# A fused Perceiver layer on one core: the attention's weight sums taken earlier on GpSimd and copied later, and a finer first load

## The chip, the core and the metric

The kernel runs on one core of a Trainium2 chip. The core has five engines with instruction streams of their own: TensorE (PE in the profile, with its weight loads as PEld) multiplies matrices, VectorE (DVE) and ScalarE (ACT) work on elements, GpSimd (POOL) does so too, and SyncE (SP) here issues DMAs. Engines wait for each other through semaphores. The metric is the device time of one execution in microseconds (us), lower is better.

## What is computed

The reference is one layer of three blocks on x (256 x 512, fp32): cross attention over 4096 context tokens and the 256 tokens themselves, a state-space block, and a mixture of experts. The change touches only the attention, cut to:

```python
q = rms_norm((ln(x) @ wq).reshape(256, 16, 128), q_norm_w)
k = rms_norm((ln(x) @ wk).reshape(256, 4, 128), k_norm_w)
v = (ln(x) @ wv).reshape(256, 4, 128)
k_ctx = rms_norm((ctx @ wk_ctx).reshape(4096, 4, 128), k_norm_w)
v_ctx = (ctx @ wv_ctx).reshape(4096, 4, 128)
q, k = rope(q), rope(k)
# keys and values of the context first, then those of x (causal)
x = x + softmax(q @ k_full.T / sqrt(128) + mask) @ v_full @ wo
```

`ln` is a layer norm without weights; 16 query heads share 4 key heads.

## The kernel before, in words

Everything is fp32. The 256 tokens are two tiles (`t`) of 128; the context is eight chunks (`c`) of 512 tokens, each of four pieces of 128.

**Loads.** SP issues the first transfers in the order written: the first piece of the first context chunk (`ctx0`, L88), the context keys' weights `wkc` in two transfers of two 128-row slices (L90 to 91), `x_sb` (L92), the rest of `ctx0` (L93, L94), and the context values' weights `wvc` (L95). `wkc` and `wvc` are the two halves of one tile `wkv`. Then come `wk`, `wq` in four column blocks, and `wv`, each in a slot of a pool of six (`wpool`, L131).

**Start.** `layernorm(t)` (L187) takes mean and variance on DVE and the inverse root on POOL (`power_half`, L181, whose POOL line is L185), then writes `xn`. Three pieces of context keys are projected (`key_piece`, L278), `xn` is transposed through PSUM into `xT` (`turn_xn`, L197), and two tables for the rotary embedding go to the first quarter of `oacc` (L388). `oacc` is the array in which the attention's output is accumulated later; its first such write is at L536.

**Queries and keys of x.** `self_block` (L429) multiplies a tile of `xT` with 512 columns of weights (PE, `ps_self`), copies the result to `raw` and squares it (ACT, L404 and L242), applies the tables (DVE, L409 to L412), and scales it by the inverse root (POOL: `r` at L185, then L413). The result is transposed (`selfT`, L437) two steps of the list at L456 later. A query block is named here by its column block and its tile, (2,1) for instance; the last, (3,0) and (3,1), end just ahead of the attention.

**Attention.** `bounded_attention` (L496) runs over stages: stage 0 for the keys of x, then one stage for each chunk. A pass of scores (`scT`, L512), the exponential on ACT, for the diagonal tiles a mask on DVE (L518), row sums on DVE, then the product with the values (`oT`, L532). In stages 1 to 7, keys and values of the next chunk are projected between these passes by a Strassen-like scheme with seven products for eight (`fast_steps`, L310). It needs four sums of blocks of the weights, T1 to T4, and four sums of blocks of each chunk, S1 to S4, all taken on POOL. `fast_weights` (L297) takes three slots of `wpool`, and writes T1, T2, T4 there and T3 in place over a block of `wkv` (L305 to L308). S1 to S4 are at L320 to L323.

**What sets the order.** A scheduler places each engine's instructions from a model of when their inputs and slots are ready; what an engine has in its stream it does in that order. SP's stream holds most DMAs, and a DMA also waits for the one that used its semaphore before it, of which there are eight.

Of the kernel before, what the change touches and what calls it, by code (L numbers as in the profile page):

```python
# [15 lines left out]
ALU = mybir.AluOpType  # L16
# [3 lines left out]
P = 128  # L20
L = 256
NT = L // P
DM = 512
KD = DM // P
T = 4096
CK = 512
NC = T // CK
NH = 16
NKV = 4
REP = NH // NKV  # L30
HD = 128
# [29 lines left out]
def rope_tables():  # L61
    inv = (1.0 / np.float32(THETA) ** (np.arange(0, HD, 2, dtype=np.float32) / np.float32(HD))).astype(np.float32)
    freqs = np.outer(np.arange(L, dtype=np.float32), inv).astype(np.float32)
    return np.stack([np.cos(freqs), np.sin(freqs)], axis=1).astype(np.float32)
# [3 lines left out]
def perceiver_layer(ctx: ExitStack, tc: tile.TileContext, a: dict, out: bass.AP):  # L68
    nc = tc.nc
    V, S, G, TE = nc.vector, nc.scalar, nc.gpsimd, nc.tensor  # L70
# [12 lines left out]
    wkv = early.tile([P, 2, KD, 512], FP, name="wkv")  # L83
    wkc, wvc = wkv[:, 0], wkv[:, 1]
    ctx0 = early.tile([P, CK // P, KD, P], FP, name="ctx0")


    load_ctx0 = lambda i, n: nc.sync.dma_start(ctx0[:, i:i + n], a["ctxT"][0, :, i:i + n])  # L88
    load_ctx0(0, 1)
    for k in range(0, KD, 2):  # L90
        nc.sync.dma_start(wkc[:, k:k + 2, :], a["wk_ctx"][k * P:(k + 2) * P, :].rearrange("(k p) n -> p k n", p=P))
    nc.sync.dma_start(x_sb, a["x"].rearrange("(t p) d -> p t d", p=P))  # L92
    load_ctx0(1, 1)  # L93
    load_ctx0(2, 2)  # L94
# [12 lines left out]
    mhalf = const.tile([P, NH], FP, name="mhalf")  # L107
# [21 lines left out]
    def layer(ctx, bounded):  # L129
# [8 lines left out]
        oacc = keep.tile([P, NT, NKV, REP * P], FP, name="oacc")  # L138
# [10 lines left out]
        def carve(tl, *shapes):  # L149

            dims = " ".join(f"d{i}" for i in range(len(tl.shape) - 1))
            tl = tl if len(tl.shape) == 2 else tl.rearrange(f"p {dims} -> p ({dims})")
            out, at = [], 0
            for shape in shapes:
                n = int(np.prod(shape))
                v = tl[:, at:at + n]
                at += n
                if len(shape) == 2:
                    v = v.rearrange("p (a b) -> p a b", b=shape[1])
                elif len(shape) == 3:  # L160
                    v = v.rearrange("p (a b c) -> p a b c", b=shape[1], c=shape[2])
                out.append(v)
            assert at <= tl.shape[1]
            return out
# [9 lines left out]
        def wpiece(src, name):  # L174

            n = src.shape[1]
            w = wpool.tile([P, KD, 512], FP, tag="w", name=name)
            nc.sync.dma_start(w[:, :, :n], src.rearrange("(k p) n -> p k n", p=P))
            return w

        def power_half(dst, src, scale, eps, n):  # L181

            v = small.tile([P, NH], FP, tag="pv", name="pv")
            V.tensor_scalar(v[:, :n], src, scale, eps, ALU.mult, ALU.add)  # L184
            G.tensor_tensor(dst, v[:, :n], mhalf[:, :n], ALU.pow)  # L185

        def layernorm(t):  # L187

            st = small.tile([P, 6], FP, tag="bn", name="bn")
            V.bn_stats(st, x_sb[:, t, :])  # L190
            mv = small.tile([P, 2], FP, tag="mv", name="mv")
            V.bn_aggr(mv, st)
            rs = small.tile([P, 1], FP, tag="rs", name="rs")
            power_half(rs, mv[:, 1:2], 1.0, 1e-5, 1)
            V.tensor_scalar(xn[:, t, :], x_sb[:, t, :], mv[:, 0:1], rs, ALU.subtract, ALU.mult)

        def turn_xn(t, tp):  # L197

            for k in range(KD):
                TE.transpose(tp[:, k * P:(k + 1) * P], xn[:, t, k * P:(k + 1) * P], ident)  # L200
            V.tensor_copy(xT[:, :, t * P:(t + 1) * P], tp.rearrange("p (k n) -> p k n", k=KD))
# [43 lines left out]
        def key_rms(raw, r):  # L245


            ss = head_squares(raw)
            if bounded:
                power_half(r, ss, 1.0, HD * 1e-6, NKV)  # L250
            else:
                power_half(r, ss, 1.0 / HD, 1e-6, NKV)
                G.tensor_tensor(raw, raw, r.unsqueeze(2).to_broadcast([P, NKV, HD]), ALU.mult)
# [40 lines left out]

        fast = {}

        def fast_weights():  # L297
            fw = [wpool.tile([P, KD, 512], FP, tag="w", name=f"fast{i}") for i in range(3)]
            T = (2, 2, 256)
            fast["T2"], fast["T4"] = carve(fw[0], T, T)  # L300
            fast["S2"], fast["S4"], fast["u3"], fast["u2"] = carve(fw[1], (2, 2, P), (2, 2, P), (2, 256), (2, 256))

            fast["T1"], fast["S1"], fast["S3"] = carve(fw[2], T, (2, 2, P), (2, 2, P))
            b11, b12, b21, b22 = (wkv[:, :, k:k + 2, n:n + 256] for k in (0, 2) for n in (0, 256))
            G.tensor_tensor(fast["T1"], b12, b11, ALU.subtract)  # L305
            G.tensor_tensor(fast["T2"], b22, fast["T1"], ALU.subtract)
            G.tensor_tensor(fast["T4"], b21, fast["T2"], ALU.subtract)
            G.tensor_tensor(b12, b22, b12, ALU.subtract)  # L308

        def fast_steps(c):  # L310
# [74 lines left out]
            return first + then[0:2] + [turn(3)] + then[2:3] + [turn(1)] + then[3:] + [turn(2), turn(0)]  # L385


        tab_q, tab_k = carve(oacc, (2, NT, HD), (2, NT, HD))  # L388
        room = carve(lacc, *[(REP, HD)] * 8)

        take_ro, take_ru = ring([room[i] for i in (0, 1, 4, 5, 7)]), ring([room[i] for i in (2, 6, 3)])
# [1 line left out]
        def rope_table(tb, w):  # L393

            half = lambda i: slice(i * HALF, (i + 1) * HALF)
            wb = [w[:, half(i)].unsqueeze(1).to_broadcast([P, NT, HALF]) for i in range(2)]
            for i in range(2):
                V.tensor_tensor(tb[:, 0, :, half(i)], rope[:, :, 0, :], wb[i], ALU.mult)
                V.scalar_tensor_tensor(tb[:, 1, :, half(i)], rope[:, :, 1, :], 2.0 * i - 1.0, wb[1 - i], ALU.mult, ALU.mult)
# [18 lines left out]
        kv[0] = (kT0, v0, None)  # L418
        ctx_k, ctx_v, ctx_t = context_pieces(0)
        for t in range(NT):  # L420
            layernorm(t)
        for i in range(3):
            ctx_k[i]()
        for t in range(NT):
            turn_xn(t, ps_sc.tile([P, 512], FP, tag="sc", name="lnT"))
        rope_table(tab_k, kw_bc)
        rope_table(tab_q, qw_bc)

        def self_block(t, w, tb, dst):  # L429
            ps = ps_mm.tile([P, 512], FP, tag="mm", name="ps_self")  # L430
            project(ps, lambda k: xT[:, k, t * P:(t + 1) * P], lambda k: w[:, k, :])
            o = norm_rope(ps.rearrange("p (h d) -> p h d", d=HD), t, tb)

            def turn():
                tp = ps_tp.tile([P, REP, P], FP, tag="tp", name="selfT")
                for h in range(REP):
                    TE.transpose(tp[:, h, :], o[:, h, :], ident)  # L437
                S.copy(dst, tp)
            return turn
# [40 lines left out]


        wo = [wpiece(a["wo"][j * 512:(j + 1) * 512, :], f"wo{j}") for j in range(3)]
        fast_weights()
        w_x = []

        def last_weights():
# [227 lines left out]
        def project_out(t):  # L714

            def piece(j):
                if j == 0:
                    m["ps_o", t] = bank("ps_o")
                for h in range(4 * j, 4 * j + 4):
                    TE.matmul(m["ps_o", t], aT[:, t, h, :], wo[j][:, h % 4, :], start=(h == 0), stop=(h == NH - 1))  # L720
                if j == 3:
                    V.tensor_tensor(x_sb[:, t, :], m["ps_o", t], x_sb[:, t, :], ALU.add)
                    layernorm(t)
            return [lambda j=j: piece(j) for j in range(4)]
# [182 lines left out]
        def mamba_out(t):  # L907
            ps = bank("ps_out")
            for k in range(DIT):
                TE.matmul(ps, m["yT", t][:, k, :], w_out[k // 4][:, k % 4, :], start=(k == 0), stop=(k == DIT - 1))  # L910
            V.scalar_tensor_tensor(x_sb[:, t, :], ps, m["ry", t], x_sb[:, t, :], ALU.mult, ALU.add)
            layernorm(t)
# [142 lines left out]
        product, series, sums = steps_of(1)  # L1055
# [284 lines left out]
    with tc.If(flag == 1) as arms:  # L1340
        with ExitStack() as lctx:
            layer(lctx, True)
    with arms.Else():
        with ExitStack() as lctx:
            layer(lctx, False)
# [12 lines left out]
def host_layout(i):  # L1358
# [7 lines left out]
        "rope": rope_tables(),  # L1366
        "W_inT": c(f[ma + "W_in"].T),
        "W_outT": c(f[ma + "W_out"].T),
        "by_channel": c(np.concatenate([f[ma + "conv_w"].reshape(XCT, P, CONV).transpose(1, 0, 2).reshape(P, XCT * CONV),
# [25 lines left out]
```

## Time and profile before

| what | us |
|---|---|
| median of 3 runs (lowest to highest) | 1034.38 (1034.35 to 1034.86) |
| profiled execution, its own time | 1035.15 |
| span of its trace, first to last instruction | 1033.4 |
| ACT busy in the span | 397.1 |
| DVE busy in the span | 476.7 |
| PE busy from 70 to 97 us | 22.37 of 27.00 |
| PE busy from 97 to 182 us | 85.00 of 85.00 |
| PE's first pass starts at | 6.04 |

Times in rows of the trace count from the span's start. In a row stand the start, the duration, the engine, the line of the code, the operation, what it writes and reads, and in brackets how long the engine had been idle before and what released it. Rows for several instructions give the time from the first start to the last end. A 128x512 matmul in fp32 appears as two passes, so a block of four has eight.

### The profile page before, as it was taken

What the parts mean: (1) busy time and instruction counts of PE and PEld (TensorE: products, weight loads), DVE (VectorE), ACT (ScalarE), POOL (GpSimd) and SP (SyncE); (2) the same over time, 40 slices, a digit from 0 to 9 for tenths busy, and PEclk for the clock granted to TensorE, in tenths of its full rate; (3) what the DMA queues carried; (4) which work ended last, traced back from release to release, by engine and by line L of the source; (5) the groups of instructions that cost most, each with busy time, mean ns of one, the idle gap of its engine ahead of it and who ended that gap; (6) DMA issues with size and microseconds to landing.
All of it is one profiled execution on the core that took longest, in us unless ns stands there. A gap on an engine that the chain in (4) does not pass through costs nothing.

```text
span 1033.4 us, 9074 instructions
## 1 busy us (share of the span) xinstructions
PE 1009.6 (98%) x2930; PEld 492.4 (48%) x2930; DVE 476.7 (46%) x947; ACT 397.1 (38%) x887; POOL 157.2 (15%) x156
## 2 busy tenths in 40 slices
PE   7998999999999999999999999999999999999997
PEld 3443444444444444444444444444556555555553
DVE  2346544344444443443543534466786563322133
ACT  3544344434444534434434434442353531222210
POOL 2374002001001100200200200000023322000022
PEclk9999999999999999999999999999999999999999
DMA  9997001000000100100100000300153457999833
GB/s 336 380 406 273 0 1 41 1 0 22 20 1 1 41 0 1 41 0 1 41 0 1 22 0 1 122 1 0 44 203 122 154 214 285 369 363 360 302 111 97
DMA packets 41499, 113.05 MB, mean 109 GB/s; under 512 B 3777, under 2 KB 4706, under 8 KB 40290
## 3 DMA queue, kind: packets, MB, share of 16 engines
q1 hardware_dynamic: 34336, 96.83, 26.0%
q0 software_dynamic: 2208, 8.39, 2.3%
q10 hardware_dynamic: 4898, 7.16, 1.9%
q8 instruction: 25, 0.41, 0.2%
q14 instruction: 32, 0.26, 0.1%
HBM read 81.42 MB, written 30.95 MB: 109 GB/s over the span
## 4 chain that ended last, share of the span: by engine, by line
PE 91%; POOL 2%; DMA 2%; DVE 2%; ACT 1%; issue 1%; SPq 0%; POOLq 0%; DVEq 0%
PE oT L532 22%; PE scT L512 22%; PE ps_kv L328 16%; PE ps_egu L206 7%; PE ps_self L206 3%; PE ps_ye L1222 2%; PE ps_o L720 2%; PE ps_xbc L206 1%; PE kTp L269 1%; PE ps_ye L1225 1%; PE ps_v L206 1%; DMA yk<-ye,row_y 1%; PE ps_out L910 1%; PE xgTp L1167 1%; PE ps_k L206 1%
## 5 line engine op out<-in xcount | busy, mean ns | idle before, releaser
L523 DVE TENSOR_TENSOR lacc<-lacc,prT 128x512 f32<-128x512 f32 x260 | 183.2, 706 | 263.1 <-ACT prT L515 263.1
L515 ACT ACTIVATE prT<-scT,bq,rk 128x512 f32<-128x512 f32 x256 | 198.3, 775 | 212.9 <-PE scT L512 208.2
L532 PE MATMUL oT<-prT,v 128*128 128x512 f32 x536 | 273.5, 592 | 0.7 <-DVE prT L518 0.7
L512 PE MATMUL scT<-qT,kT 128*128 128x512 f32 x536 | 273.6, 592 | 0.0
L532 PEld LDWEIGHTS oT<-prT,v 128*128 128x128 f32 x536 | 101.7, 190 | 128.8 <-issue 112.4
L512 PEld LDWEIGHTS scT<-qT,kT 128*128 128x128 f32 x536 | 99.0, 190 | 111.2 <-issue 110.9
L185 POOL TENSOR_TENSOR rk<-pv,mhalf 128x4 f32<-128x4 f32 x32 | 32.3, 1010 | 355.5 <-DVE pv L184 354.8
L242 ACT ACTIVATE sq<-kraw 128x128 f32<-128x128 f32 x128 | 38.2, 300 | 90.9 <-DVE kraw L346 90.9
L1182 DVE TENSOR_TENSOR hid<-si,ps_egu 128x128 f32<-128x128 f32 x32 | 9.2, 287 | 94.3 <-ACT si L1180 94.3
L328 PE MATMUL ps_kv<-wkv,fast 128*128 128x512 f32 x112 | 52.6, 592 | 0.0
L328 PE MATMUL ps_kv<-wkv,ctx 128*128 128x512 f32 x112 | 52.6, 592 | 0.0
L538 DVE TENSOR_TENSOR oacc<-oT,oacc 128x512 f32<-128x512 f32 x64 | 43.7, 683 | 1.0 <-PE oT L532 1.0
L1136 POOL DMA_INDIRECT yk<-ye,row_y x12 | 13.2, 1098 | 137.9 <-ACT si L1180 134.6
L328 PEld LDWEIGHTS ps_kv<-wkv,ctx 128*128 128x128 f32 x112 | 21.3, 190 | 26.8 <-issue 25.1
L328 PEld LDWEIGHTS ps_kv<-wkv,fast 128*128 128x128 f32 x112 | 21.3, 190 | 26.8 <-issue 23.9
L1228 ACT COPY y_sb<-ps_ye 128x512 f32<-128x512 f32 x26 | 15.3, 587 | 48.8 <-PE ps_ye L1225 43.0
L1180 ACT ACTIVATE si<-ps_egu 128x192 f32<-128x192 f32 x32 | 10.6, 332 | 58.5 <-PE ps_egu L206 58.5
L346 DVE TENSOR_TENSOR kraw<-ps_kv,fast 128x256 f32<-128x256 f32 x42 | 17.8, 424 | 30.6 <-PE ps_kv L328 30.6
L206 PE MATMUL ps_self<-wq,xT 128*128 128x512 f32 x64 | 30.3, 622 | 0.0
L720 PE MATMUL ps_o<-wo,qT 128*128 128x512 f32 x64 | 28.8, 592 | 0.0
L322 POOL TENSOR_TENSOR fast<-ctx 128x512 f32<-128x512 f32 x7 | 9.3, 1330 | 124.4 <-PE ps_kv L328 124.4
L270 ACT ACTIVATE kT<-kTp,kw_col 128x512 f32<-128x512 f32 x32 | 22.0, 688 | 14.0 <-PE kTp L269 14.0
(293 smaller groups left out, 1191.0 us busy)
## 6 DMA issues: line engine op xcount, KB each, us to landing
xg<-xn SPq DMA_DIRECT2D x6, 2560.0 KB, 21.0
w_in<-in_pairs_dram SPq DMA_DIRECT2D x14, 768.0 KB, 6.4
ctx<-in_ctxT_dram SPq DMA_DIRECT2D x7, 1024.0 KB, 4.9
xg_sb<-xg SPq DMA_DIRECT2D x28, 256.0 KB, 6.5
ye<-y_sb ACTq DMA_DIRECT2D x26, 256.0 KB, 7.0
wkv<-in_pairs_dram SPq DMA_DIRECT2D x6, 768.0 KB, 6.6
w_out<-in_pairs_dram SPq DMA_DIRECT2D x6, 768.0 KB, 6.3
oacc<-in_pairs_dram SPq DMA_DIRECT2D x6, 768.0 KB, 6.3
```

The lines of the kernel that those rows point to most:

```text
L185: G.tensor_tensor(dst, v[:, :n], mhalf[:, :n], ALU.pow)
L206: TE.matmul(ps, lhs(k), rhs_of(k), start=(k == 0), stop=(k == KD - 1))
L242: S.activation(sq[:, h, :], raw[:, h, :], AF.Square, accum_out=ss[:, h:h + 1])
L270: S.activation(kT[:, :, i * P:(i + 1) * P], tp, AF.Copy, scale=kw_col)
L328: TE.matmul(ps, lhs(k), rhs(k), start=(start and k == 0), stop=(k == 1), skip_group_check=True)
L512: TE.matmul(sc, kT[:, g, i * P:(i + 1) * P], qT[:, t, heads4(g), :].rearrange("p h q -> p (h q)"), start=True, stop=True)
L515: S.activation(pr, sc, AF.Exp, bias=shift, scale=SCALE if r is None else r[:, i, g:g + 1])
L523: V.tensor_tensor(la, la, pr, ALU.add)
L532: TE.matmul(outs[g, t], v[:, i, g * HD:(g + 1) * HD], pr, start=(n == 0), stop=last)
L538: V.tensor_tensor(ov, outs.pop((g, t)), ov, ALU.add)
L720: TE.matmul(m["ps_o", t], aT[:, t, h, :], wo[j][:, h % 4, :], start=(h == 0), stop=(h == NH - 1))
L1222: TE.matmul(ps[i], h[:, i, :], wd[:, i, :], start=True, stop=False)
```

## The change

The keys' weights come in three transfers of one, one and two slices instead of two of two. The sums T1, T2 and T4 are taken by `weight_sums`, which is called behind the rope tables, and is ordered on POOL behind the last inverse root of the first layer norm; they are written to the three quarters of `oacc` that the tables leave free. `fast_weights`, called where it was, copies them on ScalarE to the slots of `wpool` and takes only T3. The slots are divided anew: T1 and T2 in the first, T4, S1 and S2 in the second, S3, S4, u3 and u2 in the third; before, it was T2 and T4, then S2, S4, u3 and u2, then T1, S1 and S3. For the ordering, `power_half` and `layernorm` return their POOL instruction.

```diff
+    load_wkc = lambda k, n: nc.sync.dma_start(wkc[:, k:k + n, :],
+                                              a["wk_ctx"][k * P:(k + n) * P, :].rearrange("(k p) n -> p k n", p=P))
     load_ctx0(0, 1)
-    for k in range(0, KD, 2):
-        nc.sync.dma_start(wkc[:, k:k + 2, :], a["wk_ctx"][k * P:(k + 2) * P, :].rearrange("(k p) n -> p k n", p=P))
+    load_wkc(0, 1)
+    load_wkc(1, 1)
+    load_wkc(2, 2)
     nc.sync.dma_start(x_sb, a["x"].rearrange("(t p) d -> p t d", p=P))
...
-            G.tensor_tensor(dst, v[:, :n], mhalf[:, :n], ALU.pow)
+            return G.tensor_tensor(dst, v[:, :n], mhalf[:, :n], ALU.pow)
...
-            power_half(rs, mv[:, 1:2], 1.0, 1e-5, 1)
+            factor = power_half(rs, mv[:, 1:2], 1.0, 1e-5, 1)
             V.tensor_scalar(xn[:, t, :], x_sb[:, t, :], mv[:, 0:1], rs, ALU.subtract, ALU.mult)
+            return factor
...
-        def fast_weights():
+        T = (2, 2, 256)
+        b11, b12, b21, b22 = (wkv[:, :, k:k + 2, n:n + 256] for k in (0, 2) for n in (0, 256))
+
+        def weight_sums(t1, t2, t4):
+            G.tensor_tensor(t1, b12, b11, ALU.subtract)
+            G.tensor_tensor(t2, b22, t1, ALU.subtract)
+            G.tensor_tensor(t4, b21, t2, ALU.subtract)
+
+        def fast_weights(sums):
             fw = [wpool.tile([P, KD, 512], FP, tag="w", name=f"fast{i}") for i in range(3)]
-            T = (2, 2, 256)
-            fast["T2"], fast["T4"] = carve(fw[0], T, T)
-            fast["S2"], fast["S4"], fast["u3"], fast["u2"] = carve(fw[1], (2, 2, P), (2, 2, P), (2, 256), (2, 256))
-
-            fast["T1"], fast["S1"], fast["S3"] = carve(fw[2], T, (2, 2, P), (2, 2, P))
-            b11, b12, b21, b22 = (wkv[:, :, k:k + 2, n:n + 256] for k in (0, 2) for n in (0, 256))
-            G.tensor_tensor(fast["T1"], b12, b11, ALU.subtract)
-            G.tensor_tensor(fast["T2"], b22, fast["T1"], ALU.subtract)
-            G.tensor_tensor(fast["T4"], b21, fast["T2"], ALU.subtract)
+            fast["T1"], fast["T2"] = carve(fw[0], T, T)
+            fast["T4"], fast["S1"], fast["S2"] = carve(fw[1], T, (2, 2, P), (2, 2, P))
+            fast["S3"], fast["S4"], fast["u3"], fast["u2"] = carve(fw[2], (2, 2, P), (2, 2, P), (2, 256), (2, 256))
+            for n, t in zip(("T1", "T2", "T4"), sums):
+                S.copy(fast[n], t)
             G.tensor_tensor(b12, b22, b12, ALU.subtract)
...
-        tab_q, tab_k = carve(oacc, (2, NT, HD), (2, NT, HD))
+        tab_q, tab_k, *sums = carve(oacc, (2, NT, HD), (2, NT, HD), T, T, T)
...
         for t in range(NT):
-            layernorm(t)
+            normed = layernorm(t)
...
         rope_table(tab_k, kw_bc)
         rope_table(tab_q, qw_bc)
+        with tc.issue_after(normed.ins):
+            weight_sums(*sums)
...
-        fast_weights()
+        fast_weights(sums)
```

In the scheduled streams, PE's order is the same as before. POOL has the three sums right behind the layer norm's two inverse roots, then S1 and S2 between the scalings of (2,0) and (2,1), and S3, S4 and T3 between those of (3,0) and (3,1). ACT has the copy of T1 behind the copy of `selfT` that follows the second value block of x, that of T2 behind the squares of (2,0), and that of T4 between the copy of (2,1) and its squares.

## The prediction, on record before the run

> **What bounds the kernel.** I read the busy rows, the slices, the chain of waits, and then each engine's instructions in order of time. TensorE (PE) fills the span, so a change is worth what it takes out of, or puts into, PE's gaps.
>
> ```profile
> PE 1009.6 (98%) x2930; PEld 492.4 (48%) x2930; DVE 476.7 (46%) x947; ACT 397.1 (38%) x887; POOL 157.2 (15%) x156
> ...
> PE   7998999999999999999999999999999999999997
> ...
> POOL 2374002001001100200200200000023322000022
> ```
>
> The third slice (52 to 77 us) is where PE dips and POOL is busiest. The chain of waits leaves PE there (start, us, what):
>
> ```profile
> 71.23 1.33 POOL lacc L413
> 72.57 2.31 POOL fast L306
> 74.88 0.04 issue
> 74.96 2.35 POOL fast L307
> 77.31 0.98 POOL r L185
> ...
> 78.36 1.35 POOL lacc L413
> ...
> 79.75 0.66 PE selfT L437 x4
> 80.41 5.15 PE ps_self L206 x8
> ```
>
> The sums T2 and T4 (L306, L307) stand on POOL ahead of the queries' scaling (r at L185, lacc at L413), for which the transpose selfT waits. PE's own rows:
>
> ```profile
> 72.62 0.66 PE L437 MATMUL selfT<-ident,lacc 128*128 128x128 f32 x4 [0.52 <-POOL lacc L413]
> 73.12 3.60 PE L206 MATMUL ps_self<-wq,xT 128*128 128x512 f32 x8
> 79.75 0.66 PE L437 MATMUL selfT<-ident,lacc 128*128 128x128 f32 x4 [3.04 <-POOL lacc L413]
> 80.25 5.29 PE L206 MATMUL ps_self<-wq,xT 128*128 128x512 f32 x8
> ```
>
> Eight passes take 3.60 and then, behind the gap, 5.29. The windows say why (us, then PE's busy time, ..., granted clock third from the end):
>
> ```profile
> 80.00:82.00 2.00, 2.00 (x7) 0.97 (x6) 0.25 (x1) 1.55 (x8) 0.00 (x0) 0.73 1.05 410
> 82.00:84.00 2.00, 2.00 (x4) 0.84 (x3) 0.17 (x1) 0.21 (x2) 1.36 (x2) 0.50 1.05 410
> ```
>
> The clock was halved behind the gap.
>
> **The loss there now.** Starts follow each other by 3.44 us for a block of eight passes, 0.44 for four transposes, 0.43 for a pass of scT or oT. Without waits the first selfT would start at 68.51 + 3.44 = 71.95. From there to the scores at 94.68 PE needs 4 x 0.44 + 3 x 3.44 + 8 x 0.43 = 15.52 us and takes 22.73. The 7.2 are: 0.67 before selfT of query block (2,0) [group 2, token tile 0]; 3.19 before that of (2,1); 1.69 of half clock; 0.90 where oT waits for DVE's mask L518; 0.60 before selfT of (3,1); 0.17 of slower starts behind waits.
>
> **Part 1: T1, T2, T4 move from about 63 to 77 us to behind the first layer norm on POOL.** They read both weights, so they wait for the values' weights: issued at 6.38, landed 9.0 later, 15.4. Three instructions of 2.35 (rows L305 to L307) end at about 22.5. Queued behind them are two rk (1.01 each, first used by the second attention stage), the memset of xn (its reader, the first clearing of xg, issues at 31.77), and the first r at 30.29. POOL is done with all by 26. Cost 0; the cover is 4 us deep.
>
> Beside them DVE makes the copies xT<-lnT (L201, two of 0.69 at 19.06), needed at 23.16. [...]L364, which also reads PSUM, took its 0.69 at 166.14 under POOL's L322. I take 0 by the row.
>
> **Part 2: three ScalarE copies of 128x1024.** Copies of 256, 384 and 512 columns took 0.375, 0.484 and 0.587; 0.105 per 128 more gives 1.01. In ACT's new order the first stands behind qT at 61.44, in a gap up to 64.83; the second behind the squares ending at 67.07, in a gap up to 68.71; the third behind raw of (2,1), so that block's squares end about 1 us later (71.5), which DVE's rope of that block hides (below). Without such a gap each would cost 1.0. Cost 0. Their slots are those of wv and wq2, free at 60.9 and 68.7, before each copy.
>
> **Part 3: the queries' scaling comes earlier.** An undisturbed block is (0,0): raw at 38.60, scaled at 43.59, 4.99 later. So (2,0), raw at 64.83, is scaled at 69.82, before 71.95: 0.67 gone.
>
> Behind it now stand S1 and S2 (1.27 each, 69.85 on), where S1 and S3 stood at 65.3. They meet the rope of (2,1) on DVE[...]: L410 took 1.48 instead of 0.42 under L322, and ended 0.28 behind it; L409 ended 0.55 behind L320. In turns: L409 to 70.4, S1 to 71.5, L410 to 71.8, S2 to 72.9, L411 to 73.2, L412 to 73.9; then r to 75.05 and L413 to 76.16. selfT of (2,1) is wanted at 71.95 + 0.44 + 3.44 = 75.83 and starts at 76.21: a wait of 0.38 stays of 3.19.
>
> A gap of 0.4 should not halve the clock. [...]The row has 0.50 right behind that gap, and 5.29 for a block of 3.60. I take the row: 1.69 gone.
>
> **Part 4: what is late next.** (3,0) is now scaled late relative to PE: raw 76.04, but its squares wait for the copy of the selfT at 76.21; L413 ends at about 81.05. The block (3,1) ends on PE at 76.21 + 0.50 + 3.44 + 0.17 = 80.3. S3, S4 and T3 (L308) follow on POOL, as S2, S4, T3 do now, but 0.9 later against that block (then they began at 85.63, 0.1 behind it). Turns again: L409 to 81.6, S3 to 82.8, L410 to 83.0, S4 to 84.2, L411 to 84.5, T3 (2.35) to 86.7, L412 to 87.2, mask L518 to 87.8. oT is wanted at 76.71 + 2 x 3.44 + 0.44 + 6 x 0.43 = 86.6 and starts at 87.85: 1.2 (0.90 before). L413 of (3,1), behind T3, r (1.43) and DVE's copies (1.11 as now), ends at about 89.35; the last selfT is wanted at 88.7 and starts at 89.4: 0.7 (0.60 before). The scores follow at 89.9 instead of 94.68: **4.8 us earlier**. All later PE work keeps its order and moves with it.
>
> **Part 5: the first transfers.** SP issues one more DMA (0.43 to 0.47 each), and the eight semaphores of the DMAs shift by one: the second piece of ctx0 now waits for the landing of the first (0.79 + 3.6 = 4.4) instead of going at 2.73; the third waits for rope (6.35). The first 256 KB of the keys' weights should land between ctx0 (4.4) and the present 512 KB (1.23 + 4.7 = 5.9), say 5.2, so PE starts 0.8 earlier[...]. But the second key block waits now for ctx0's second piece:
>
> ```profile
> PEld ps_k L206 <- DMA ctx<-in_ctxT_dram: 1.0, 1, 1.0
> ```
>
> It starts at 11.45, and that data stands behind x_sb (landed 10.7) in either kernel. Bounds: a gain of 0.4 if the piece comes 0.4 sooner; a loss of 1.3 if, issued at 4.45, it takes the 8.3 of ctx0's third piece and lands at 12.75. I take 0: it is queued behind the same bytes.
>
> **Sum.** Parts 1, 2, 5: 0. Parts 3 and 4: 7.2 - (0.38 + 1.2 + 0.7 + 0.12 for starts) = 4.8. The span goes from 1033.4 to 1028.6, the profiled execution from 1035.15 to 1030.35; the median lies 0.77 below that execution, so 1034.38 becomes **1029.6 us**.
>
> **Rivals.**
> - *The half clock comes back at the attention's opening.* [...]Price 1.7: 1031.3. Chance 0.15.
> - [...]nearly all waits go: up to 7.2, 1027.2. For it: (1,0) and (1,1) pass with no wait. Against: T3 stays where it was. Chance 0.10.
> - *Slower: the second piece of ctx0 lands late.* Issued at 4.45 and with the 10.1 of wk, it lands at 14.55: 3.1 of idle PE, and 1.7 of half clock behind it, 4.8 in all, which eats the gain; that is the point from which this decides. With the 12.8 of wv: 17.25, 5.8 + 1.7 = 7.5 lost, 1037.1. Against: those were queued behind more bytes. Chance 0.06.
> - *The sums are no help*, since S1 and S2 in front of (2,1) hold POOL as long: that wait stays 3.2 and the clock drops, leaving 0.7: 1033.7. The two are 2.5 against 4.7 us for T2 and T4, and begin 2.7 earlier. Chance 0.04.
>
> The forecast has 0.65. Its own range is 1028.4 to 1030.9 (part 5 from -0.4 to 1.3, turns 0.8). With the better turns and the clock, 1027.3 to 1032.2. 0.2% is 2.1 us, about what a measurement here tells from no change: faster 0.88, same 0.06, slower 0.06.
>
> **What would show it.** selfT's wait for lacc near 76 under 0.8 and granted clock 1.00 from 76 to 92; POOL's three oacc rows at 15.4 to 22.5; ps_self at 23.2 unmoved; oT's first wait 1 to 1.5; the second key block at 11.45. It is wrong if the wait at 76 is over 2, if half clock shows after 20 us, or if ps_k's wait for ctx grows by more than 1.

## The result, and the profile after

| | us |
|---|---|
| before, median of 7 runs (lowest to highest) | 1034.64 (1034.35 to 1035.94) |
| after, median of 7 runs | 1030.59 (1030.25 to 1032.96) |
| ratio after / before, 95% interval | 0.9961 (0.995 to 0.9973) |
| profiled execution, before and after | 1035.15 and 1030.59 |
| span, before and after | 1033.4 and 1028.8 |
| scores of stage 0 behind the last `selfT`, before and after | 94.68 and 90.08 |

The change makes the kernel 4.05 us faster by the medians, 4.6 us by the two profiled executions. The span shrank by 4.6 us, and all of it lies ahead of the attention's second run of scores. The line numbers of the kernel after are larger: `selfT` is L447, the scaling L421 (its root L188), the rope L417 to L420, the mask L528, `scT` L522, `oT` L542, T3 L316.

PE's rows of the kernel after, in order of time (start, duration, engine and line, what, and in brackets the idle time before with what ended it):

```profile
71.98 0.60 PE L447 MATMUL selfT<-ident,lacc 128*128 128x128 f32 x4
...
76.31 0.66 PE L447 MATMUL selfT<-ident,lacc 128*128 128x128 f32 x4 [0.30 <-POOL lacc L421]
76.81 3.60 PE L210 MATMUL ps_self<-wq,xT 128*128 128x512 f32 x8
...
88.13 1.13 PE L542 MATMUL oT<-prT,v 128*128 128x512 f32 x2 [1.28 <-DVE prT L528]
89.59 0.66 PE L447 MATMUL selfT<-ident,lacc 128*128 128x128 f32 x4 [0.33 <-POOL lacc L421]
90.08 1.02 PE L522 MATMUL scT<-qT,kT 128*128 128x512 f32 x2
```

The wait of 0.52 at 72 us has gone, that of 3.04 has become 0.30, and the block behind it takes 3.60 again instead of 5.29. What is left is where the attention opens, and there the first wait has grown: `oT` waits 1.28 for the mask. PE's rows of the kernel before, at the same place:

```profile
92.73 1.12 PE L532 MATMUL oT<-prT,v 128*128 128x512 f32 x2 [0.74 <-DVE prT L518]
...
94.68 1.02 PE L512 MATMUL scT<-qT,kT 128*128 128x512 f32 x2
```

POOL and DVE show why. POOL's rows of the kernel after:

```profile
81.21 1.74 POOL L330 TENSOR_TENSOR fast<-ctx 128x512 f32<-128x512 f32 x1
82.91 1.46 POOL L331 TENSOR_TENSOR fast<-ctx,fast 128x512 f32<-128x512 f32 x1
84.32 2.53 POOL L316 TENSOR_TENSOR wkv<-wkv 128x1024 f32<-128x1024 f32 x1
```

And DVE's, of the same kernel and the same stretch:

```profile
83.16 1.49 DVE L419 TENSOR_TENSOR lacc<-raw,oacc 128x256 f32<-128x256 f32 x1
84.57 2.31 DVE L187 TENSOR_SCALAR pv<-ss 128x4 f32<-128x4 f32 x1
86.80 0.68 DVE L420 TENSOR_TENSOR lacc<-lacc 128x512 f32<-128x512 f32 x1
87.40 0.68 DVE L528 TENSOR_TENSOR prT<-prT,upper 128x512 f32<-128x512 f32 x1
```

Each rope operation of 128x256, 0.42 when it is alone, takes 1.49 here and ends 0.28 behind the POOL sum that it meets. During T3 DVE does nothing but an operation on four columns (2.31, elsewhere 0.17), and the rest of the rope and the mask come behind it. `oT` starts when the mask is done.

### The profile page after: what moved, and what is told of

The parts are those of the page before. It is cut to its first block, busy times and chain, and to the rows that moved or that the text cites. A ratio compares the mean times of both kernels' runs of the same rounds, so it can differ in the third digit from the quotient of the medians.

```text
span 1028.8 us, 9081 instructions
## 1 busy us (share of the span) xinstructions
PE 1008.2 (98%) x2930; PEld 491.6 (48%) x2930; DVE 480.7 (47%) x947; ACT 399.6 (39%) x890; POOL 155.8 (15%) x156
## 4 chain that ended last, share of the span: by engine, by line
PE 91%; DVE 3%; DMA 2%; POOL 2%; issue 1%; ACT 1%; SPq 0%; POOLq 0%; DVEq 0%
PE oT L542 22%; PE scT L522 22%; PE ps_kv L336 16%; PE ps_egu L210 7%; PE ps_self L210 3%; PE ps_ye L1232 2%; PE ps_o L730 2%; PE kTp L273 1%; PE ps_ye L1235 1%; PE ps_v L210 1%; PE ps_k L210 1%; PE ps_out L920 1%; PE xgTp L1177 1%; PE ps_xbc L210 1%; PE total L1223 1%
## 5 line engine op out<-in xcount | busy, mean ns | idle before, releaser
L542 PE MATMUL oT<-prT,v 128*128 128x512 f32 x536 | 273.5, 592 | 1.3 <-DVE prT L528 1.3
L522 PE MATMUL scT<-qT,kT 128*128 128x512 f32 x536 | 273.6, 592 | 0.0
L542 PEld LDWEIGHTS oT<-prT,v 128*128 128x128 f32 x536 | 101.7, 190 | 129.3 <-issue 112.6
L522 PEld LDWEIGHTS scT<-qT,kT 128*128 128x128 f32 x536 | 99.0, 190 | 111.2 <-issue 110.9
L188 POOL TENSOR_TENSOR rk<-pv,mhalf 128x4 f32<-128x4 f32 x32 | 32.3, 1011 | 351.8 <-DVE pv L187 351.1
L336 PE MATMUL ps_kv<-fast,fast 128*128 128x512 f32 x112 | 52.6, 592 | 0.0
L336 PEld LDWEIGHTS ps_kv<-fast,fast 128*128 128x128 f32 x112 | 21.3, 190 | 26.8 <-issue 21.8
```

Of the source, the lines that this page charges most:

```text
L188: return G.tensor_tensor(dst, v[:, :n], mhalf[:, :n], ALU.pow)
L336: TE.matmul(ps, lhs(k), rhs(k), start=(start and k == 0), stop=(k == 1), skip_group_check=True)
L522: TE.matmul(sc, kT[:, g, i * P:(i + 1) * P], qT[:, t, heads4(g), :].rearrange("p h q -> p (h q)"), start=True, stop=True)
L542: TE.matmul(outs[g, t], v[:, i, g * HD:(g + 1) * HD], pr, start=(n == 0), stop=last)
```

## The experiments

Every ratio is to the kernel before, run beside the experiments in three sets; its medians there were 1035.19 (27 runs, the first four experiments), 1034.46 (15 runs, the next three) and 1034.96 (9 runs, the last two).

The theory going in: all of the gain comes from T1, T2 and T4 being off POOL's stream from 63 to 77 us, and a part of it, 1.7 us, from PE's clock; the finer load does nothing; T3 holds what is left. Against it stood that the load brought a part, and that the long block of 5.29 us was not the gap's doing.

**The sums alone.** The kernel after, with the load of before:

```diff
-    load_wkc(0, 1)
-    load_wkc(1, 1)
-    load_wkc(2, 2)
+    for k in range(0, KD, 2):
+        nc.sync.dma_start(wkc[:, k:k + 2, :], a["wk_ctx"][k * P:(k + 2) * P, :].rearrange("(k p) n -> p k n", p=P))
```

> The changed kernel with the old first transfers (two of two slices). My theory: the finer first load is worth nothing, since the second key block waits for the second piece of ctx0 in either kernel. Time within 0.3 us of the changed kernel's 1030.6; the first block starts near 6.0 and the transposes of xn near 18.4. Rival (the finer load gives part of the gain): 0.4 to 0.8 us more than the changed kernel.

Measured: 1031.54 (1030.45 to 1031.65), ratio 0.9965 (0.9953 to 0.9978), where the whole change has 0.9961. The median is 0.95 above that of the change, more than the 0.3 expected; the runs of before beside it were 0.55 slower as well, so the times leave some tenths open. In the trace PE starts at 6.01 instead of 5.50, and from 72 us on its waits are those of the kernel after: 0.30, 1.28, scores at 90.15 instead of 90.08.

**The load alone.** The kernel before, with the finer load (the diff above, turned round):

> The kernel before with the finer first transfers alone. My theory: within 0.3 us of before (1034.6), PE starting at 5.5 and waiting for the third transfer and for ctx0 all the same. Rival (the finer load gives part of the gain): 0.4 to 0.8 us less.

Measured: 1034.58 (1032.93 to 1036.34), ratio 0.9999 (0.9991 to 1.0007). PE starts at 5.39, 0.65 earlier. Its profiled execution keeps 0.5 of it up to the transposes of `xn` (17.91, before 18.42); that of the kernel after, with the same load, keeps nothing (18.46). PE's rows of the start of the kernel after show where it goes:

```profile
5.50 3.75 PE L210 MATMUL ps_k<-wkv,ctx 128*128 128x512 f32 x4 [5.50 <-DMA wkv<-in_wk_ctx_dram]
9.45 4.02 PE L210 MATMUL ps_k<-wkv,ctx 128*128 128x512 f32 x8 [0.19 <-DMA wkv<-in_wk_ctx_dram]
```

The first four passes take 3.75, because the third waits for the second transfer up to 7.0, and the last of the three transfers lands at about 9.4, where the second of two landed at 8.5 before. The second key block, which waits for the second piece of `ctx0`, starts at 11.48 (11.45 before, 10.93 in the kernel with the load alone). Over all eleven profiles the transposes start at 17.91 to 18.48 with the finer load (six, median 18.36) and at 18.42 to 19.03 without it (five, median 18.53). So the finer load is worth about 0.2 us by the traces, less than their spread, and makes no difference that the times can tell.

**The gap filled.** Is it the gap that halves the clock? The kernel before, with six passes that compute nothing that is used, put into the gap:

```diff
+        def then_fill(f):
+            turn = f()
+            ps = ps_sc.tile([P, 512], FP, tag="sc", name="fill")
+            for k in range(3):
+                TE.matmul(ps, ident, wkc[:, k, :], start=True, stop=True)
+            return turn
+
+        q[3][0] = lambda f=q[3][0]: then_fill(f)
```

> The kernel before with three matmuls of 128x512 added to PE behind query block (3,0), into a PSUM tile that nothing reads: they run in PE's gap ahead of the transpose of (2,1) and leave every wait of it as it is. If the half clock behind the gap comes from PE's idle time (my theory), granted clock stays 1.00 and the 1.7 us of the slow block go: 1032.9. If the clock falls for another reason (the rival[...]), the time stays at 1034.6 or grows by up to 0.9.

PE's rows of this kernel, behind the six passes that end at 79.91:

```profile
80.38 0.66 PE L437 MATMUL selfT<-ident,lacc 128*128 128x128 f32 x4 [0.47 <-POOL lacc L413]
80.87 3.60 PE L206 MATMUL ps_self<-wq,xT 128*128 128x512 f32 x8
```

`selfT` is as late against the rows ahead of it as before, but the block behind it takes 3.60. That is one execution, and alone it shows little, since the half clock is not there in every execution of before either. Over the three sets 24 of its 51 runs have a mean granted clock of 0.999 or 1.000 and take 1033.39 to 1035.06; the other 27 have 0.995 to 0.998 and take 1034.56 to 1038.42. The profiled execution of before had the half clock, and that of the load alone, with a gap of 2.74, had the full clock throughout. What counts is the clock of all runs: with the gap filled none of 14 lies below 0.998, where 17 of those 51 do (0.998 itself can come from elsewhere, since five of the 14 have it too). So the long block was the gap's doing. The time is 1033.85 (1033.23 to 1036.19), ratio 0.9989 (0.9981 to 0.9998): 1.3 us, less than the 1.7 expected, since part of the executions of before had nothing to lose.

**T3 moved.** What does T3 cost where the attention opens? The kernel after, with T3 behind the last scaling on POOL, all else as it was:

```diff
+        scaled = []
...
-            G.tensor_tensor(b12, b22, b12, ALU.subtract)
+            with tc.issue_after(scaled[-1].ins):
+                G.tensor_tensor(b12, b22, b12, ALU.subtract)
...
-            G.tensor_tensor(o, o, r.unsqueeze(2).to_broadcast([P, REP, HD]), ALU.mult)
+            scaled.append(G.tensor_tensor(o, o, r.unsqueeze(2).to_broadcast([P, REP, HD]), ALU.mult))
```

> The changed kernel with T3 ordered on POOL behind the scaling of the last query block instead of ahead of its inverse root. My theory: what is left of the loss at the attention's opening is T3[...]; the first wait of oT (1.28) and the last selfT's (0.33) go, scores at about 88.0 instead of 90.08, then up to 0.4 is given back where a later mask meets T3: 1.7 less than the changed kernel, about 1028.9. Rival (the wait only moves, because T3 meets the masks of the first stage in full): within 0.4 of 1030.6.

Measured: 1029.2 (1028.62 to 1030.71), ratio 0.9947 (0.9935 to 0.9958). PE's rows of this kernel:

```profile
86.70 1.08 PE L544 MATMUL oT<-prT,v 128*128 128x512 f32 x2
87.61 0.60 PE L449 MATMUL selfT<-ident,lacc 128*128 128x128 f32 x4
88.05 1.02 PE L524 MATMUL scT<-qT,kT 128*128 128x512 f32 x2
```

Both waits are gone, and the scores come at 88.05 instead of 90.08. T3 now starts at 87.46 and holds DVE's copies of the first exponentials for 3.54 instead of 1.61 us; the mask behind them is late, and the third pair of `oT` passes starts at 90.93, 0.3 after PE was free. Three runs of scores later 93.69 stands against 95.23 in the kernel after, so 0.5 of the 2.0 us is given back.

**All chunk sums moved too.** If late is good for T3, is it for S1 to S4? The kernel above, and:

```diff
-            sums()
+            with tc.issue_after(scaled[-1].ins):
+                sums()
```

> The changed kernel with T3 and the first chunk's S1 to S4 all ordered on POOL behind the scaling of the last query block; only T1, T2, T4 stay early. My theory[...]: no wait of selfT or oT up to the scores, which start near 87.5 (90.08 in the changed kernel); then 7.4 us of sums meet the masks of the first attention stage and give back 0.5 to 1.5. 1.0 to 2.0 us less than the changed kernel, as much as with T3 alone or 0.4 better. Rival (each sum that moves behind costs a mask its whole length there): slower than with T3 alone by 1 us or more.

Measured: 1030.91 (1030.79 to 1031.75), ratio 0.9963 (0.995 to 0.9977): nothing over the kernel after, so the gain that was expected did not come. The wait for lacc at 76 us is gone (`selfT` at 75.73), and everything is 0.6 earlier, but then T3 starts at 84.87, just ahead of the mask. DVE's rows of this kernel:

```profile
85.25 2.51 DVE L531 TENSOR_TENSOR prT<-prT,upper 128x512 f32<-128x512 f32 x1 [2.32 <-ACT prT L528]
87.90 2.68 DVE L534 COPY lacc<-prT 128x512 f32<-128x512 f32 x2
```

The first mask takes 2.51 for 0.68, and `oT` waits 1.60, later 0.34 and 0.29. In the kernel with T3 alone moved, T3 missed the first mask, because S3 and S4 had held the last scaling back to 87.5.

**No early sums, only a late place.** Would the order alone have done? The kernel before, with T1, T2, T4, T3 and S1 to S4 all behind the last scaling:

```diff
-            G.tensor_tensor(fast["T1"], b12, b11, ALU.subtract)
-            G.tensor_tensor(fast["T2"], b22, fast["T1"], ALU.subtract)
-            G.tensor_tensor(fast["T4"], b21, fast["T2"], ALU.subtract)
-            G.tensor_tensor(b12, b22, b12, ALU.subtract)
+            with tc.issue_after(scaled[-1].ins):
+                G.tensor_tensor(fast["T1"], b12, b11, ALU.subtract)
+                G.tensor_tensor(fast["T2"], b22, fast["T1"], ALU.subtract)
+                G.tensor_tensor(fast["T4"], b21, fast["T2"], ALU.subtract)
+                G.tensor_tensor(b12, b22, b12, ALU.subtract)
```

The sums of the chunk are put behind it in the same way.

> The kernel before with all of its sums, T1 to T4 and the first chunk's S1 to S4, ordered on POOL behind the scaling of the last query block; no early sums, no copies on ACT, old first transfers. If only the place ahead of the queries' scaling costs time (the rival to the early sums being needed), the waits go here too: scores near 87.5 and a time near that of the all-late changed kernel, about 1029. My theory: 14.5 us of POOL work then stand in the first attention stage[...], and the masks are late several times: 2 to 5 us given back, 1029.5 to 1032.5, slower than the changed kernel with everything else late.

Measured: 1036.96 (1036.43 to 1041.08), ratio 1.0025 (1.0014 to 1.0035), slower than before, where 1029.5 to 1032.5 was expected. The 3.04 at `selfT` is gone, and in its place stand three waits for the mask, of 1.61, 2.51 and 1.39. PE's rows of this kernel:

```profile
87.92 1.13 PE L535 MATMUL oT<-prT,v 128*128 128x512 f32 x2 [1.61 <-DVE prT L521]
...
94.57 1.33 PE L535 MATMUL oT<-prT,v 128*128 128x512 f32 x2 [2.51 <-DVE prT L521]
95.70 1.91 PE L515 MATMUL scT<-qT,kT 128*128 128x512 f32 x2
```

The passes behind the second wait run at half clock (two passes take 1.91 for 1.02; the granted clock is 0.50 from 95.67 to 99.08), and all 11 runs have a mean clock of 0.998 or less. The expectation had the late masks, but not the half clock behind them. So the sums do have to leave this stretch: this later place only moves the wait from `selfT` to `oT`.

**The kernel after, once more**, beside the last two:

> The changed kernel again, unaltered, to stand beside the two others on one chip. About 4 us less than before; no half clock in the middle of any execution, so mean clocks of 0.998 to 1.000, while part of the executions of before show 0.997 or less.

Measured: 1030.69 (1030.21 to 1031.13), ratio 0.9958 (0.9944 to 0.9971).

**Early without array and copies.** By the theory the sums need only an early, idle stretch of POOL, so the copies and the attention output's array are not essential: if `fast_weights` asks for its slots before `wo` does, they are those of `wk` and the first two blocks of `wq`, free at about 31, 42 and 57 us. The kernel before, with its own load, and:

```diff
-            fast["T2"], fast["T4"] = carve(fw[0], T, T)
-            fast["S2"], fast["S4"], fast["u3"], fast["u2"] = carve(fw[1], (2, 2, P), (2, 2, P), (2, 256), (2, 256))
-
-            fast["T1"], fast["S1"], fast["S3"] = carve(fw[2], T, (2, 2, P), (2, 2, P))
+            fast["T1"], fast["T2"] = carve(fw[0], T, T)
+            fast["T4"], fast["S1"], fast["S2"] = carve(fw[1], T, (2, 2, P), (2, 2, P))
+            fast["S3"], fast["S4"], fast["u3"], fast["u2"] = carve(fw[2], (2, 2, P), (2, 2, P), (2, 256), (2, 256))
...
+            s1, s2, s3, s4 = chunk_sums(ctx_tiles[1])
+            with tc.issue_after(scaled[3].ins):
+                G.tensor_tensor(fast["T1"], b12, b11, ALU.subtract)
+                G.tensor_tensor(fast["T2"], b22, fast["T1"], ALU.subtract)
+                G.tensor_tensor(fast["T4"], b21, fast["T2"], ALU.subtract)
+                s1()
+            with tc.issue_after(scaled[5].ins):
+                s3()
+                s2()
+                s4()
...
-        wo = [wpiece(a["wo"][j * 512:(j + 1) * 512, :], f"wo{j}") for j in range(3)]
         fast_weights()
+        wo = [wpiece(a["wo"][j * 512:(j + 1) * 512, :], f"wo{j}") for j in range(3)]
```

`chunk_sums` returns the four sums of a chunk as functions; later chunks take them where they did. S1 to S4 of the first chunk move forward here too, so what the weights' sums and what these are worth is not told apart.

> The kernel before with its own loads, no sums in the attention output's array and no copies on ScalarE. Instead the six buffers of the sums take the first three weight slots that come free (those of wk, wq0 and wq1, free at about 31, 42 and 57 us) ahead of the three loads of wo, so the sums can be made where they stay. T1, S1, T2, T4 are ordered behind the scaling of query block (0,1) (POOL idle from 47.9 to 56.8), S3, S2, S4 behind that of (1,1) (idle from 63.1 to 67.7), T3 alone stays between the scalings of (3,0) and (3,1). Theory (the loss lies only in what POOL does ahead of the scalings near 72, 76 and 89 us, and early sums need no copies if slots are free early enough): no selfT wait over 0.4 us at 72, 76 and 89, T3 done by about 84 and ahead of the mask, oT waits 0.3 or less, scores near 88; against the changed kernel 1.5 to 2.5 us less, against the one before 0.9938 to 0.995. Rival ([...]the waits only change place): T4 holds the rope of (1,0), S3 to S4 hold that of (2,0), T3 the mask; scores at 90 or later, ratio 0.996 to 0.998. Second rival: the loads of wo, now behind these, come late; then the output projection after 740 us would wait for weights.

Measured: 1028.28 (1027.84 to 1028.43), ratio 0.9934 (0.9921 to 0.9948). PE's rows of this kernel from the first `selfT` that had waited:

```profile
72.19 0.60 PE L445 MATMUL selfT<-ident,lacc 128*128 128x128 f32 x4
...
76.06 0.60 PE L445 MATMUL selfT<-ident,lacc 128*128 128x128 f32 x4
...
86.38 1.08 PE L540 MATMUL oT<-prT,v 128*128 128x512 f32 x2
87.46 0.66 PE L445 MATMUL selfT<-ident,lacc 128*128 128x128 f32 x4
87.96 1.02 PE L520 MATMUL scT<-qT,kT 128*128 128x512 f32 x2
```

No row of this stretch has a wait in brackets, those left out neither. From 72.19 to the scores are 15.77 us, where 15.52 of work stand without any wait. POOL's rows of this kernel show where the sums went, and where T3 ended up:

```profile
48.03 2.34 POOL L307 TENSOR_TENSOR fast<-wkv 128x1024 f32<-128x1024 f32 x1
...
53.99 2.35 POOL L309 TENSOR_TENSOR fast<-wkv,fast 128x1024 f32<-128x1024 f32 x1
...
81.90 2.52 POOL L315 TENSOR_TENSOR wkv<-wkv 128x1024 f32<-128x1024 f32 x1 [0.58 <-PE ps_v L206]
```

T1, T2 and T4 are done by 56.3, and T3 has POOL to itself from 81.90 to 84.4. It still stretches one rope operation of (3,1) to 2.57 us, for 0.42 alone, but it is over before the mask at 85.59. The second rival did not show: the output projection, which reads `wo`, starts at 704.5, 2.1 earlier than in the kernel after.

**T3 alone moved, once more**, on the same chip as the kernel just shown:

> The changed kernel with T3 alone behind the last scaling, once more, on the chip of e7: scores at 88.0 as before, ratio 0.9947 within 0.0010. If the loss of the changed kernel at the attention's opening is what T3 does there, it is again 1.0 to 1.7 us faster than the changed kernel was.

Measured: 1028.99 (1028.19 to 1029.19), ratio 0.994 (0.9927 to 0.9954). The two versions are 0.7 us apart; their ranges overlap a little (one run of five, at 1028.19, lies in the other's range). In both the scores come at 88.0 instead of 90.08, and both ratios are below those of the change as made (0.9961 and 0.9958). The interval of T3 alone meets both of those intervals, that of the other version meets one.

## Why the prediction was right, point by point

It said 1029.6 us, and 1028.6 for the span; measured were 1030.59 and 1028.8.

- **Part 1** (sums early, at no cost): they ran from 15.46 to 22.68, and POOL was done at 26.07. The copies of `xT`, which read PSUM, took 1.29 for the two beside T2 (2 x 0.69, which overlap a little). The row by which this was chosen, L364, is a `tensor_tensor` and no copy; the outcome is the same.
- **Part 2** (ScalarE's copies hidden): they took 1.06, 1.04 and 1.05 where 1.01 was worked out, at 61.96, 67.01 and 69.23, in the gaps named. No wait on PE comes from them.
- **Part 3** (`selfT` near 76): the start was 76.31 instead of 76.21, and the wait fell from 3.04 to 0.30. The turns of DVE and POOL ahead of it came as worked out: L418 and L419 took 1.49 each beside S1 and S2, for 0.42 alone. The clock is 1.00 from 76 to 92, and the block behind the wait of 0.30 took 3.60, so the 1.69 went, as the row had it. Some executions of the same kernel pay for the gap and some don't (before: a mean clock of 0.995 to 0.998 in 27 of 51 runs, of 0.999 or 1.000 in 24). What differs between them was not shown.
- **Part 4** (T3 is late next): `oT` started at 88.13 for 87.85, the last `selfT` at 89.59 for 89.4, the scores at 90.08 for 89.9. The waits came about as worked out; in one detail it was another instruction: the working had T3 hold back the rope's last operation (L412, now L420), but `pv` stands ahead of that one, and it was `pv` that T3 held; the rest of the rope and the mask came behind it all the same. Moving T3 took out both waits.
- **Part 5** (finer load, at no gain): the two kernels that have only one half of the change each agree with it, within some tenths. PE started at 5.50 where 5.2 was worked out. The first passes run at half pace: the weight loads of before start 0.85 apart from 7.03 to 8.74 and 0.43 apart from 9.43 on, although the granted clock reads 1.00 there.

**The term that was mis-sized** is the last one of the sum: "the median lies 0.77 below that execution". Taken from the trace, the step from one profiled execution to the other was 4.8 and measured 4.56. But the profiled execution of before had paid for the half clock (mean clock 0.997), and about half of its executions have not; the kernel after has a profiled execution that is its median, and nothing is to be subtracted. That is 0.77 of the 1.0 us by which the forecast is off; the other 0.24 is mostly the waits of parts 3 and 4, where the scores came 0.18 later than worked out. The set with the kernel after once more shows the two kinds side by side: 8 runs of before at a clock of 0.999 or 1.000 have a median of 1034.03, 3.3 above the 1030.69 of after; the other 7 have 1035.67, 5.0 above. They are 1.65 apart (1.5 in the other two sets), near the 1.69 of the long block. A median over both kinds lies in between, and moved 4.05 in one set and 3.8 in the other. None of the 12 runs of the kernel after has a mean clock below 0.999.

Of the rivals, the half clock did not come back at the attention's opening: it reads 1.00 there, as a window of the kernel after shows (us, busy time of PE, PEld, DVE, ACT and POOL, granted clock, share and rate of the DMAs):

```profile
84.50:88.00 3.50, 2.35 (x6) 0.76 (x4) 3.50 (x4) 2.51 (x4) 3.39 (x2) 1.00 1.05 409
```

That nearly all waits go did not come by itself, but can be had: the version that asks for its slots first brings the scores to 87.96, 6.7 of the 7.2 us. The slow second piece of `ctx0` did not happen: it was issued at 4.59 instead of 2.73, and the block that reads it started at 11.48 for 11.45. Nor were the early sums of no help: the wait behind S1 and S2 is 0.30.

## What to carry to other kernels

Elementwise work on POOL can cost twice: it delays what is queued behind it there, and it held many of the DVE operations on SBUF that ran beside it until it ended (here a mask took 2.51 for 0.68 us, an operation on four columns 2.31 for 0.17); so it belongs where DVE has nothing urgent, and a place that is merely later can meet something worse. Before data are staged and copied, see whether the final buffers can be had earlier by asking for them in another order. If a profiled execution shows a reduced clock behind a gap, look at the mean clock of other executions before its full price is carried over to the median.

## What the runs showed of the hardware that was not expected

**A tiny operation can be held for a whole large one.** `pv`, a `tensor_scalar` of 128x4, took 2.31 us beside T3, where it takes 0.17 alone; with T3 moved, the same instruction took 0.16. It is so under the early sums as well, where nobody waits for it. DVE's rows of the kernel after, beside the sums at 15.46, 17.89 and 20.33:

```profile
15.82 2.09 DVE L187 TENSOR_SCALAR pv<-ss 128x4 f32<-128x4 f32 x2
19.09 1.29 DVE L205 COPY xT<-lnT 128x512 f32<-128x512 f32 x2 [1.19 <-PE lnT L204]
20.59 2.12 DVE L187 TENSOR_SCALAR pv<-ss 128x4 f32<-128x4 f32 x1 [0.20 <-ACT sq L246]
```

Four columns in SBUF wait out the first and the third sum (2.09 for two of them, 2.12 for one), while 512 columns from PSUM pass beside the second at full pace (1.29 for two of 0.69). So the small operation was held and the large one was not; what decides it was not shown. A `tensor_scalar` of 128x1 in the kernel before, at 813.36 beside POOL's L884, took its 0.14.

**The half clock came neither in every execution nor behind every gap.** In the profiled execution of before it lasts from 80.94 to 84.35, in the kernel with all sums late about twice as long. Windows that show it (columns as in the window above; the first two are of before, the next three of the kernel with all sums late, the last is of the kernel with the load alone):

```profile
77.53:80.94 3.41, 1.19 (x6) 0.88 (x7) 2.69 (x4) 0.49 (x2) 2.09 (x2) 1.00 1.05 408
80.94:84.35 3.41, 3.41 (x5) 1.35 (x4) 0.17 (x1) 1.27 (x9) 1.71 (x2) 0.50 1.05 409
...
92.25:95.67 3.42, 1.10 (x2) 0.49 (x3) 3.42 (x3) 0.59 (x1) 3.42 (x2) 0.96 0.84 325
95.67:99.08 3.41, 2.02 (x4) 0.42 (x2) 3.38 (x3) 0.69 (x1) 3.41 (x3) 0.50 0.02 9
99.08:102.50 3.42, 3.42 (x4) 1.11 (x5) 3.42 (x4) 0.00 (x0) 2.40 (x2) 0.55 0.00 0
...
75.50:79.00 3.50, 0.76 (x3) 0.06 (x2) 2.07 (x3) 0.59 (x1) 3.31 (x3) 1.00 1.05 407
```

PE was busy 1.19 of 3.41 us ahead of the half clock in before, and 1.10 of 3.42 where it began in the kernel with all sums late. In the kernel with the load alone it was busy 0.76 of 3.50, around its gap of 2.74, and the clock stayed at 1.00 (the next 3.50 us too). With the gap filled none of 14 runs was below 0.998, so the half clock there takes the gap; what else it takes was not shown.
